# Batch 1's first graph layer run in lent tiles beside batch 0's later layers, nodes normalised in place, planner constants set anew

## The chip, the cores and the metric

The kernel runs on one core of one Trainium2 chip. The metric is the device time of one execution in microseconds, as a median of several runs. The core has TensorE (PE; its weight loads are PEld), VectorE (DVE), ScalarE (ACT), GpSimd (POOL) and SyncE (SP), which here only issues DMAs.

## The reference

Sixteen graphs (batches) of 1024 nodes with 256 features share one 0/1 adjacency matrix `adj`. Four layers follow each other, each with a normalisation ahead of it and a residual sum behind it:

```python
h = jnp.maximum(_layernorm(x, axis=-1), 0.0)
x = x + _L0_gnn_ref(h, adj, W0, a0)   # graph attention, 4 heads of 64
h = jnp.maximum(_layernorm(x, axis=-1), 0.0)
x = x + _L1_gnn_ref(h, adj, W1, a1)   # graph attention, 1 head of 256
h = jnp.maximum(_layernorm(x, axis=-1), 0.0)
x = x + _L2_gnn_ref(h, adj, W2, a2)   # graph attention, 1 head of 256
h = jnp.maximum(_layernorm(x, axis=-1), 0.0)
x = x + _L3_gnn_ref(h, adj, ...)      # 8 heads of 32 with q, k, v, then a feed-forward
# a graph layer:
q = h @ W; e = leaky_relu(q @ a_src + (q @ a_dst).T); e = where(adj > 0, e, -big)
out = act(softmax(e) @ q)
# the last layer:
t = softmax(where(adj > 0, q @ k.T / sqrt(32), -1e9)) @ v
y = layernorm(h + t); y = layernorm(y + relu(y @ w1 + b1) @ w2 + b2)
```

All of it is in float32. Only the kernel's branch `direct` matters here; another branch, `general`, isn't executed with these inputs.

## The kernel before

**Tiling.** A batch's 1024 nodes are eight tiles of 128, and most steps work on a half of four tiles (512 nodes). One half of a batch's nodes is one tile `xt` of a ring of three. For the last layer the normalised nodes go into halves `hna` of another ring of three, and the attention's result and the feed-forward's first normalisation are made in them.

**The stages of a batch.** `batch(b)` loads the nodes (L1537), takes their sums and squares on ACT (L1547, L429), runs `gat` for the three graph layers, writes the nodes to DRAM as `x3` (L1568), runs `attention`, then `feed`, which reads `x3` back as `xr` for the residual sum (L1444).

**A graph layer.** `gat` normalises a half into `hn` (ACT, L483), transposes it to `hT`, multiplies by the weights widened by the score columns (L716) and takes exponentials of the scores (L727). A leaky-ReLU softmax weight is then a maximum of a row and a column term: a row of scores is transposed, written to DRAM (`rd`, L789) and read back spread over all partitions (`row`, L797), and DVE makes each masked tile of weights `pt` from it in one instruction (L813). In the first layer, with four heads, TensorE multiplies in column-tiled form, four 32-column products side by side (L927), with the denominators (L937); in the other two one 257-column product does both (L840). One tile `qb` holds the projected nodes of a layer, so that a layer's products must be through before the next layer's projection writes it, whichever batch that is of.

**The attention.** `project` makes queries and keys of four heads (L1077), splits each into a high part `hi` (ACT, L1086) and a low part `lo` (DVE, L1089) of which there is one buffer each, and SP copies these by sixteen 64 KB DMAs into stacked tiles `ks` and `qs` (L1098). The 32 steps of a batch each make four score tiles `sc` (TensorE, L1295), their exponentials `pa` (ACT, L1319), the mask (DVE, L1328) and the products with the values in column-tiled form (L1161); the denominators come from sums of `pa`, partly by DVE (L1188), partly by accumulating DMAs from POOL's queue (L1196), and in the last batch from `pa` themselves. The four `sc` banks are taken in turn by scores, projections and transposes of this stage; four other PSUM banks serve everything else.

**The order.** Nothing is issued as the code runs. Every operation is put on record with its engine, an estimated duration, and what it reads and writes, and `schedule` then plays the program through: on each engine it takes, among the operations that can start soonest, the one with the lowest key, and issues them in that order. The key of an operation is its batch number plus a value between knots along the stage (`GATS`, `VALUES`, `STEPS`, `FEED`), less a `LEAD` for ACT and DVE. `SWITCH` is what a turn of TensorE between its kinds of products costs ("col4" is column-tiled, "qk" scores, "full" the rest); it is added to the duration, and times `BIAS` to the key when TensorE's next operation is chosen. A DMA takes its issue time on its queue, and its result counts as there when the queue's earlier transfers and its own are through, plus `LANDING`. On the chip each engine then does its list in this order, and waits where the plan was wrong.

Of the kernel before, what the change touches and what calls it, by code (L numbers as in the profile page):

```python
# [82 lines left out]

class Shared(Ring):
# [14 lines left out]
PASS = {"pe": 0.22, "act": 0.18, "dve": 0.15, "pool": 0.13, "dma": 0.0}  # L99


class Work:


    def __init__(self, engine, us, emit, key, modes, moved):
        self.engine, self.us, self.emit, self.key, self.modes = engine, us, emit, key, modes
        self.pass_on = PASS[engine]
        self.moved = moved
        self.before = {}
        self.after = []  # L110
        self.shared = []
        self.opens = []
        self.ready = 0.0
        self.left = 0
# [10 lines left out]
class Record:  # L125
# [12 lines left out]
    def add(self, engine, us, emit, w=(), r=(), modes=("full", "full"), key=None, moved=0.0):  # L138
        stream = self.streams[-1]
        x = Work(engine, us, frozen(emit), key, modes, moved)  # L140
# [29 lines left out]
    def schedule(self):  # L170
# [8 lines left out]
        queue = dict.fromkeys(PASS, 0.0)  # L179
# [22 lines left out]
        def choose(e):  # L202
# [10 lines left out]
            if future[e] and (best is None or future[e][0][0] < best[0]):  # L213
                t, n, x = future[e][0]
                if opening(x) is not None:
                    t = max(t, at, opening(x))
                    best = min(best or (1e9,), (t, x.key + turn(x), n, x))
# [3 lines left out]
        while True:  # L221
# [18 lines left out]
            if x.moved:  # L240
                queue[e] = max(at + 0.2, queue[e]) + x.moved
                x.pass_on = queue[e] + LANDING - (at + us)
# [17 lines left out]
LANDING = 2.8  # L260
BIAS = 0.939
LEAD = {"act": 2.715, "dve": 0.501}

SWITCH = {
    ("full", "col4"): 0.095,
    ("full", "col2"): 0.095,
    ("qk", "full"): 0.104,
    ("qk", "col4"): 0.2,
    ("qk", "col2"): 0.2,
    ("col4", "full"): 0.135,  # L270
    ("col4", "qk"): 0.135,
    ("col4", "col2"): 0.135,
    ("col2", "full"): 0.1,
    ("col2", "qk"): 0.1,
# [3 lines left out]
def act_us(n, pointers=0):  # L278
    return (n / 1.2 + 65 + 93 * pointers) / 1000


def tt_us(n):
    return (n / 0.96 + 73) / 1000


def stt_us(n):
    return (n / 0.96 + 130) / 1000


def ts_us(n):  # L290
    return (n / 0.96 + 56) / 1000


def mm_us(n):
    return 2 * max(2 * n / 2.4 + 2.3, 109) / 1000
# [5 lines left out]
def direct(ctx, tc, flag, x, adj, gat_w, gat_a, w_qkv, ln1_g, ln1_b, ln2_g, ln2_b, w1, b1, w2, b2, out):  # L301
# [10 lines left out]

    GATS = (
        (-3.456, -2.901, -1.928, -0.561, 0.293),
        (0.136, 0.471, 0.668, 0.738, 0.779),
        (0.851, 0.853, 0.845, 0.944, 1.195),
    )
    VALUES = (1.183, 1.195, 1.056, 1.638, 0.894)
    STEPS = (1.054, 1.508, 1.709, 1.977, 2.039)
    FEED = (2.172, 2.298, 2.316, 2.334, 2.401)  # L320
# [34 lines left out]
    r_xt = ring("xt", 3, [TH, C])  # L355
# [13 lines left out]
    r_hna = ring("hna", 3, [TH, C])  # L369
# [43 lines left out]
    def dma(moved, emit, w, r, key=None, us=0.44, engine="dma"):  # L413
        rec.add(engine, us, emit, w, r, key=key, moved=moved)

    def stats(src, src_ref, dst, dst_ref, whose="g"):
        st = r_st[whose].new()
        dve(0.342, lambda: nc.vector.bn_stats(st.t, src), [st], [src_ref])
        dve(0.11, lambda: nc.vector.bn_aggr(dst, st.t), [dst_ref], [st])
# [3 lines left out]
    def spread_of(srcs, src_refs, sums, squares, refs):  # L423

        act(0.19, lambda: nc.scalar.mul(sums, sums, -1.0 / C), refs, [])
        for k, (src, src_ref, ref) in enumerate(zip(srcs, src_refs, refs)):
            act(
                act_us(C, 1) + 60e-3,
# [51 lines left out]
    def normal(dst, dst_ref, src, src_ref, bias, scale, refs, func):  # L480
        act(
            act_us(C, 2),
# [5 lines left out]
    def watch(b_rec, view, k):  # L488
# [4 lines left out]
            0.3,  # L493
# [39 lines left out]
    def prepare(l):  # L533
# [5 lines left out]
            1.1,  # L539
# [7 lines left out]
            0.5,  # L547
            lambda: nc.sync.dma_start(
# [49 lines left out]
    def neighbours(it):  # L598
# [3 lines left out]
            1.9, lambda: nc.sync.dma_start(a_i, adj[it * P : (it + 1) * P, :]), [a32], []  # L602
# [39 lines left out]
    def setup():  # L642
# [3 lines left out]
        for it in range(NT):  # L646
# [5 lines left out]
            3.2,  # L652
            lambda: nc.sync.dma_start(wqkv_sb, w_qkv.rearrange("(t p) d -> p t d", p=P)),
# [12 lines left out]
        dma(5.0, load_feed, [b_feed], [], us=3.6)  # L666
# [4 lines left out]
    def gat(xt, b_mv, b_rstd, l):  # L671
# [3 lines left out]
        b_qb, b_e3, b_rec = r_qb.new(), r_e3.new(), r_rec.new()  # L675
# [4 lines left out]
        for hf in range(2):  # L680
# [5 lines left out]
            hn, hT = r_hn.new(), r_hT.new()  # L686
# [24 lines left out]
            for k, it in enumerate(its):  # L711
                g = r_bank.new()

                def project():
# [11 lines left out]
                    0.184,  # L726
# [30 lines left out]
            if H == 1:  # L757
                act(
                    0.17,
# [5 lines left out]
                0.4,  # L765
# [10 lines left out]
        def turn_rows(hf):  # L776

            g, rt, rd = r_bank.new(), r_rt.new(), r_rd.new()
# [9 lines left out]
            act(0.17, lambda: nc.scalar.copy(rt.t[:n, :], g.t[:n, :P]), [rt], [g])  # L788
            dma(0.15, lambda: nc.sync.dma_start(rd.t[:n, :], rt.t[:n, :]), [rd], [rt])  # L789
            return rd  # L790

        def spread(hf, h, rd):

            row = r_row.new()
            dma(
                1.4,
# [11 lines left out]
        def weights(hf, h, jt, row):  # L808

            pt = r_pt.new()  # L810
# [17 lines left out]
        for hf in range(2):  # L828
            s = slice(hf * TH, (hf + 1) * TH)
            if H == 1:  # L830
                row = spread(hf, 0, rds[hf])
                pts = [weights(hf, 0, jt, row) for jt in range(NT)]
                for k in range(TH):
                    it = hf * TH + k
                    g = r_bank.new()
                    for j0 in range(0, NT, PART):
# [22 lines left out]
                        0.116,  # L859
# [4 lines left out]
                    b_ex = r_ex.new()  # L864
# [7 lines left out]
                    if l != 1:  # L872
# [8 lines left out]
                            act_us(C),  # L881
# [10 lines left out]
                    else:  # L892
# [3 lines left out]
                        stt_us(C) + 60e-3,  # L896
# [15 lines left out]
            for h in range(0, H, 2):  # L912
                row = [spread(hf, h + u, rds[hf]) for u in range(2)]
                g, gd = r_bank.new(), r_bank.new()
                for jt in range(0, NT, 2):
# [7 lines left out]
                    def product():  # L923
# [23 lines left out]
                        3 * 0.855,  # L947
# [8 lines left out]
                for ac in (g, gd):  # L956
                    ot = r_ot.new()
# [13 lines left out]
                b_o, b_ex = r_ex.new(), r_ex.new()  # L971
# [5 lines left out]
                def sums():  # L977
# [9 lines left out]
                dve(0.13, lambda: nc.vector.reciprocal(r, r), [ref], [])  # L987
# [11 lines left out]
                act(act_us(HALF), lambda: nc.scalar.activation(ex, o, AF.Exp), [b_ex], [b_o])  # L999
                act(  # L1000
                    act_us(HALF),
# [25 lines left out]
    def attention(b, xt, b_mv, b_rstd):  # L1027
        rec.stream(b, VALUES)
        mv, rstd = b_mv.t, b_rstd.t
        hn, hT, va = Halves(r_hna), r_hTa.new(), r_va.new()  # L1030
# [39 lines left out]
        def project(g, hf, keys, stack, at):  # L1070
# [22 lines left out]
            for a in range(4):  # L1093
                part = ((hi, hi, lo, lo), (hi, lo, hi, lo))[keys][a]
                for r in range(HG):
                    dma(
                        0.33,
# [6 lines left out]
                        us=0.635,  # L1104
# [68 lines left out]
        rec.stream(b, STEPS)  # L1173
# [1017 lines left out]
```

## Time and profile before

| what | value |
|---|---|
| runs | 4154.15, 4158.94, 4161.55 us (median 4158.94) |
| span of the profiled execution | 4150.3 us |
| mean granted TensorE clock | 0.991 |
| busy, share of the span | PE 98%, PEld 57%, DVE 84%, ACT 65%, POOL 13% |
| DMA | 389.63 MB, 22.3% of the 16 engines' time from SP's queue, 16.0% from POOL's |
| scores of batch 0 | first end at 230 us |
| scores of batch 14 and 15 | 3740 to 3958 us, 3988 to 4110 us |
| from one batch's scores to the next | some 252 us |

The profiled execution is given by its span, from the first to the last instruction; the median of the runs lies 8.6 us above it. A busy time is the union of an engine's instructions in the trace. A matmul's row is as long as its stay in the pipeline, so that the rows of TensorE overlap; where it matters, the distance between the ends of two matmuls is used. A float32 product of the reference's full precision shows as two records.

### The profile page before, as it was taken

What the parts mean: (1) busy time and instruction counts of PE and PEld (TensorE: products, weight loads), DVE (VectorE), ACT (ScalarE), POOL (GpSimd) and SP (SyncE); (2) the same over time, 40 slices, a digit from 0 to 9 for tenths busy, and PEclk for the clock granted to TensorE, in tenths of its full rate; (3) what the DMA queues carried; (4) which work ended last, traced back from release to release, by engine and by line L of the source; (5) the groups of instructions that cost most, each with busy time, mean ns of one, the idle gap of its engine ahead of it and who ended that gap; (6) DMA issues with size and microseconds to landing.
All of it is one profiled execution on the core that took longest, in us unless ns stands there. A gap on an engine that the chain in (4) does not pass through costs nothing.

```text
span 4150.3 us, 68028 instructions
## 1 busy us (share of the span) xinstructions
PE 4049.7 (98%) x23874; PEld 2358.5 (57%) x23874; DVE 3504.5 (84%) x5994; ACT 2680.9 (65%) x6673; POOL 558.7 (13%) x631
## 2 busy tenths in 40 slices
PE   7899999999999999999999999999999999999998
PEld 3746556564665646556464665646556465564643
DVE  7498888988889898898988889888897988889866
ACT  4556667576766756667566665756667566575665
POOL 0001111111111101111111111111111111111110
PEclk9999999999999999999999999999999999999999
DMA  3124444344443424443254443434434244442441
GB/s 105 37 67 103 116 96 102 77 90 105 100 109 84 103 78 100 114 105 95 69 112 108 97 102 88 92 92 100 110 92 100 71 103 119 98 95 65 98 111 47
DMA packets 215246, 389.63 MB, mean 94 GB/s; under 512 B 45168, under 2 KB 80240, under 8 KB 214896
## 3 DMA queue, kind: packets, MB, share of 16 engines
q1 hardware_dynamic: 180336, 259.36, 22.3%
q0 software_dynamic: 34560, 125.84, 16.0%
q8 instruction: 190, 3.11, 0.3%
q14 instruction: 160, 1.31, 0.1%
HBM read 91.03 MB, written 33.95 MB: 30 GB/s over the span
## 4 chain that ended last, share of the span: by engine, by line
PE 79%; ACT 8%; DVE 6%; DMA 2%; SPq 2%; issue 2%; POOL 0%; DVEq 0%; ACTq 0%
PE bank L840 18%; PE bank L1161 12%; PE sc L1295 10%; PE bank L927 10%; PE bank L716 7%; PE bank L512 5%; PE bank L937 5%; PE bank L1392 5%; PE sc L1077 4%; ACT waste L429 2%; PE sc L1113 2%; SPq L1098 2%; DVE pa L1328 2%; ACT pa L1319 1%; DVE pt L813 1%
## 5 line engine op out<-in xcount | busy, mean ns | idle before, releaser
L1319 ACT ACTIVATE pa<-sc 128x512 f32<-128x512 f32 x2048 | 1108.1, 607 | 448.7 <-PE sc L1295 317.5
L1328 DVE TENSOR_TENSOR pa<-pa,mask 128x1024 f32<-128x1024 f32 x1024 | 1221.9, 1220 | 72.9 <-ACT pa L1319 68.6
L813 DVE SCALAR_TENSOR_TENSOR pt<-row,e,mask 128x512 f32<-128x512 f32 x1536 | 1068.1, 747 | 49.6 <-DMA row<-rd 35.8
L840 PE MATMUL bank<-qb,pt 128*128 128x257 f32 x4096 | 943.9, 383 | 1.4 <-DVE pt L813 1.0
L840 PEld LDWEIGHTS bank<-qb,pt 128*128 128x128 f32 x4096 | 780.5, 191 | 143.8 <-ACT pa L1319 11.7
L1295 PE MATMUL sc<-qs,ks 128*128 128x512 f32 x2048 | 702.8, 451 | 39.1 <-DVE lo L1089 35.7
L1295 PEld LDWEIGHTS sc<-qs,ks 128*128 128x128 f32 x2048 | 361.2, 190 | 288.1 <-issue 91.2
L1161 PE MATMUL bank<-pa,va 128*32 128x512 f32 x4096 | 514.7, 597 | 1.3 <-DVE pa L1328 1.0
L927 PE MATMUL bank<-pt,qb 128*32 128x512 f32 x4096 | 502.2, 596 | 4.3 <-DVE pt L813 3.4
L1188 DVE TENSOR_TENSOR sums<-pa,pa 128x1024 f32<-128x1024 f32 x360 | 435.6, 1221 | 30.3 <-PE bank L1161 25.3
L716 PE MATMUL bank<-w_aug,hT 128*128 128x259 f32 (+1 forms) x1536 | 391.2, 393 | 2.1 <-ACT hT L710 1.9
L1196 POOL DMA_DIRECT2D sums<-pa x240 | 210.5, 877 | 1059.4 <-DVE rec L860 239.0
L716 PEld LDWEIGHTS bank<-w_aug,hT 128*128 128x128 f32 x1536 | 283.9, 192 | 110.3 <-ACT pa L1319 12.6
L868 ACT ACTIVATE ex<-bank,rec 128x256 f32<-128x256 f32 x256 | 123.4, 482 | 303.3 <-DVE rec L860 302.6
L927 PEld LDWEIGHTS bank<-pt,qb 128*32 128x32 f32 x4096 | 122.3, 109 | 296.5 <-issue 224.0
L937 PE MATMUL bank<-pt,e 128*32 128x512 f32 x2048 | 278.6, 594 | 0.0
L1161 PEld LDWEIGHTS bank<-pa,va 128*32 128x32 f32 x4096 | 116.4, 109 | 256.7 <-issue 216.9
L1077 PE MATMUL sc<-hTa,wqkv_sb 128*128 128x512 f32 x512 | 244.5, 602 | 1.6 <-ACT pa L1319 0.8
L483 ACT ACTIVATE hn<-xt,mv,rstd 128x256 f32<-128x256 f32 x384 | 203.3, 597 | 51.6 <-DVE mv L456 30.0
L429 ACT ACTIVATE waste<-xt,mv 128x256 f32<-128x256 f32 x384 | 196.2, 511 | 7.0
L1161 PE MATMUL bank<-sums,ones 128*32 128x512 f32 x1440 | 193.5, 599 | 0.2 <-DMA sums<-pa 0.2
L1086 ACT CAST hi<-sc 128x512 fp32r<-128x512 f32 x128 | 74.5, 582 | 178.9 <-PE sc L1077 76.9
(119 smaller groups left out, 4305.9 us busy)
## 6 DMA issues: line engine op xcount, KB each, us to landing
sums<-pa POOLq DMA_DIRECT2D x240, 512.0 KB, 5.9
row<-rd SPq DMA_DIRECT2D x192, 256.0 KB
ks<-hi SPq DMA_DIRECT2D x512, 64.0 KB
ks<-lo SPq DMA_DIRECT2D x512, 64.0 KB
qs<-hi SPq DMA_DIRECT2D x512, 64.0 KB
qs<-lo SPq DMA_DIRECT2D x512, 64.0 KB
xt<-in_x_dram SPq DMA_DIRECT2D x32, 512.0 KB
x<-xt SPq DMA_DIRECT2D x32, 512.0 KB
```

What stands on the lines that cost most here:

```text
L429: lambda: nc.scalar.activation(waste.t, src, AF.Square, bias=sums[:, k : k + 1], accum_out=squares[:, k : k + 1]),
L716: nc.tensor.matmul(g.t[:, : C + 3 * H], hT.t[:, ct, k * P : (k + 1) * P], w_aug[l][:, ct, :], start=ct == 0, stop=ct == CT - 1,)
L813: lambda: nc.vector.scalar_tensor_tensor(pt.t, row.t, e3[:, 2, jt // TH, h, jt % TH : jt % TH + 1], mask[:, jt, hf * HALF : (hf + 1) * HAL ...
L840: nc.tensor.matmul(g.t[:, : D + 1], pts[jt].t[:, k * P : (k + 1) * P], qb[:, jt, 0, :], start=jt == 0, stop=jt == NT - 1,)
L927: nc.tensor.matmul(g.t[u * D + d : u * D + d + D3, :], qb[:, j, h + u, d : d + D3], pts[u][j - jt].t, start=j == 0, stop=j == NT - 1,)
L937: nc.tensor.matmul(gd.t[c : c + D3, :], one(jt + k, h + u).to_broadcast([P, D3]), pts[u][k].t, start=jt == 0, stop=jt == NT - 2,)
L1077: nc.tensor.matmul(sc.t, wqkv_sb[:, ct, c0 : c0 + P], hT.t[:, ct, hf * HALF : (hf + 1) * HALF], start=ct == 0, stop=ct == CT - 1,)
L1161: nc.tensor.matmul(ac.t[r * D3 : (r + 1) * D3, :], columns(r), of_head(r), start=first, stop=last,)
L1188: lambda: nc.vector.tensor_add(ss.t, p0.t, p1.t),
L1295: nc.tensor.matmul(scs[r - r0].t, ks.t[:, r, jt * P : (jt + 1) * P].bitcast(F32R), q.t[:, r, :].bitcast(F32R), start=True, stop=True,)
L1319: lambda: nc.scalar.activation(pt.t[:, v, :], sc.t, AF.Exp, scale=1.0 / math.sqrt(D3)),
L1328: lambda: nc.vector.tensor_mul(pt.t, pt.t, mask[:, jt : jt + 1, i0 : i0 + HALF].to_broadcast([P, 2, HALF]),),
```

## The change

It has four parts.

1. **The first graph layer of batch 1 in lent tiles.** `gat` takes its tiles from a set of rings `my`. `own` is the set as before. `lent()` makes another out of tiles that the attention and the feed-forward use (`va`, `hTa`, `xr`, `yT`, `fz`, `sums`, two of the six `pa`), which stand idle before the first attention. Batch 1's first layer is recorded right behind batch 0's, in the lent tiles, with knots of its own ("beside"); then the tiles are given back, and the next users of them wait for its instructions. Every later batch's layers use the own tiles, as before.
2. **Nodes in place.** `hna` is gone; `xt`'s ring has six halves and is named `xh`. The last layer's normalised nodes overwrite the nodes in `xh`, once the copy to `x3` has read them.
3. **The planner's model of a DMA.** SP and POOL share one queue of transfers, each transfer has its own landing time, and the issue of one takes as long as the queue is more than `AHEAD` = 3.5 us ahead. An operation that is to become ready may be taken ahead of an earlier one whose PSUM banks aren't free.
4. **New constants.** The estimated durations of operations, the cost of a turn, `BIAS`, `LEAD` and all knots are new; batch 15's feed-forward has knots of its own ("last").

The diff, cut to what matters:

```diff
+class Lent(Ring):
+    def __init__(self, tiles, owners):
+        super().__init__(tiles)
+        self.owners = owners
+    def new(self):
+        buf = super().new()
+        if len(self.bufs) <= len(self.tiles):
+            buf.parts[None][1] = [y for o in self.owners for y in o.parts[None][1]]
+        return buf
+    def give_back(self):
+        for o in self.owners:
+            o.uses += [y for buf in self.bufs for y in buf.uses]
...
             if future[e] and (best is None or future[e][0][0] < best[0]):
-                t, n, x = future[e][0]
-                if opening(x) is not None:
-                    t = max(t, at, opening(x))
-                    best = min(best or (1e9,), (t, x.key + turn(x), n, x))
+                for t, n, x in sorted(future[e]):
+                    if opening(x) is not None:
+                        t = max(t, at, opening(x))
+                        best = min(best or (1e9,), (t, x.key + turn(x), n, x))
+                        break
...
             if x.moved:
-                queue[e] = max(at + 0.2, queue[e]) + x.moved
-                x.pass_on = queue[e] + LANDING - (at + us)
+                queue = max(at + (us if e == "pool" else 0.2), queue) + x.moved
+                us = max(us, queue - at - AHEAD)
+                x.pass_on = queue + x.lands + SLACK - (at + us)
...
-LANDING = 2.8
-BIAS = 0.939
-LEAD = {"act": 2.715, "dve": 0.501}
+AHEAD = 3.5
+SLACK = 0.56
+KNOTS = {
+    "gat0": (-6.706, -3.534, -2.307, -1.522, -2.815),
+    "gat1": (0.005, 0.503, 0.618, 0.731, 0.916),
+    "gat2": (0.938, 0.468, 0.637, 0.867, 1.15),
+    "beside": (0.241, 1.203, 1.943, 0.54, 4.121),
+    "values": (1.06, -3.362, -0.305, 3.145, 0.767),
+    "steps": (1.014, 1.448, 1.59, 2.064, 1.794),
+    "feed": (2.016, 2.165, 2.509, 2.154, 2.609),
+    "last": (2.808, 3.335, 3.547, 5.206, 6.138),
+}
+BIAS = 1.225
+LEAD = {"act": 9.55, "dve": -0.732}
 SWITCH = {
-    ("full", "col4"): 0.095,
...
-    ("qk", "full"): 0.104,
-    ("qk", "col4"): 0.2,
...
-    ("col4", "full"): 0.135,
-    ("col4", "qk"): 0.135,
...
+    ("full", "col4"): 0.137,
+    ("col4", "full"): 0.18,
+    ("qk", "col4"): 0.15,
+    ("col4", "qk"): 0.184,
+    ("qk", "full"): 0.016,
 }
...
-    GATS = (
-        (-3.456, -2.901, -1.928, -0.561, 0.293),
-        (0.136, 0.471, 0.668, 0.738, 0.779),
-        (0.851, 0.853, 0.845, 0.944, 1.195),
-    )
-    VALUES = (1.183, 1.195, 1.056, 1.638, 0.894)
-    STEPS = (1.054, 1.508, 1.709, 1.977, 2.039)
-    FEED = (2.172, 2.298, 2.316, 2.334, 2.401)
...
-    r_xt = ring("xt", 3, [TH, C])
+    r_xh = ring("xh", 6, [TH, C])
...
-    r_hna = ring("hna", 3, [TH, C])
...
+    def lent():
+        va, hTa, xr = r_va.new(), r_hTa.new(), r_xr.new()
+        yT, fz, sums, pa = ([r.new() for _ in range(2)] for r in (r_yT, r_fz, r_sums, r_pa))
...
+        rings = types.SimpleNamespace(
+            qb=Lent([va.t.rearrange("p t c -> p (t c)")], [va]),
+            hn=Lent([wide[:, 0, :].rearrange("p (t c) -> p t c", c=C)], [hTa]),
+            hT=Lent([wide[:, 1, :].rearrange("p (t n) -> p t n", n=HALF)], [hTa]),
+            row=Lent(both(yT[:1]), yT[:1]),
...
+            rd=ring("rdl", 2, [P], dram),
+            pt=Lent(both(sums + pa), sums + pa),
+            ex=Lent(both(yT[1:]), yT[1:]),
+            ot=Lent([b.t for b in fz], fz),
+        )
+        return rings
...
-    def gat(xt, b_mv, b_rstd, l):
+    def gat(xt, b_mv, b_rstd, l, my):
...
-        b_qb, b_e3, b_rec = r_qb.new(), r_e3.new(), r_rec.new()
+        b_qb, b_e3, b_rec = my.qb.new(), my.e3.new(), my.rec.new()
...
     def attention(b, xt, b_mv, b_rstd):
-        hn, hT, va = Halves(r_hna), r_hTa.new(), r_va.new()
+        hn, hT, va = xt, r_hTa.new(), r_va.new()
...
     setup()
+    states = [begin(0), begin(1)]
+    graph(0, states[0], 0)
+    borrowed = lent()
+    graph(0, states[1], 0, borrowed, KNOTS["beside"])
+    for r in vars(borrowed).values():
+        if isinstance(r, Lent):
+            r.give_back()
     for b in range(NB):
-        batch(b)
+        if b > 1:
+            states.append(begin(b))
+        for l in range(int(b < 2), 3):
+            graph(b, states[b], l)
+        end(b, states[b])
```

`begin` is the first part of `batch` (load, sums, squares), `graph` sets the knots and calls `gat`, `end` is the rest: the copy to `x3`, `attention` and `feed`.

## The prediction, made before the change was run

> **What bounds the kernel now.** I read the page first, then the windows, then TensorE's own waits.
>
> ```profile
> PE 4049.7 (98%) x23874; PEld 2358.5 (57%) x23874; DVE 3504.5 (84%) x5994; ACT 2680.9 (65%) x6673; POOL 558.7 (13%) x631
> PE   7899999999999999999999999999999999999998
> DVE  7498888988889898898988889888897988889866
> PE 79%; ACT 8%; DVE 6%; DMA 2%; SPq 2%; issue 2%; POOL 0%; DVEq 0%; ACTq 0%
> ```
>
> TensorE bounds it: busy 98% of the span, 79% of the chain. But a busy row is not a full one. I multiply each matmul group's record count by the usual distance between ends in an unbroken run of it: 4096 x 217 ns (L840's, the second and third layer's products), 2048 x 232 ns (scores), 9888 column-tiled records (L927, L937, L1161: four heads or parts side by side, eight records of such a quad end within 0.85 us) at 107 ns, 1024 x 429 ns (L1077, L1392), 1024 x 219 and 512 x 226 ns (projections), 512 x 216 ns (values), 2720 transposes at 109 ns. That is 3825 us. So 4150 - 3825 = **325 us** is what a reordering could at best win. The windows show where it sits.
>
> ```profile
> 0.00:50.00 50.00, 31.65 (x182) 19.95 (x186) 36.23 (x84) 30.66 (x90) 5.14 (x12) 0.97 0.54 186
> 50.00:100.00 50.00, 46.27 (x357) 14.82 (x350) 42.24 (x79) 11.56 (x20) 1.01 (x1) 0.97 0.09 32
> 100.00:150.00 50.00, 43.19 (x194) 35.57 (x193) 20.73 (x59) 21.12 (x58) 3.41 (x6) 0.90 0.04 12
> 150.00:200.00 50.00, 45.62 (x194) 36.54 (x192) 21.75 (x60) 30.90 (x96) 3.49 (x6) 0.90 0.15 46
> 200.00:250.00 50.00, 47.92 (x321) 22.61 (x325) 38.13 (x65) 24.92 (x64) 3.26 (x5) 1.00 0.42 118
> 250.00:300.00 50.00, 48.27 (x340) 20.88 (x332) 49.05 (x79) 29.88 (x64) 6.25 (x4) 1.00 0.13 33
> 4000.00:4050.00 50.00, 46.98 (x262) 17.59 (x262) 37.15 (x44) 32.21 (x71) 1.72 (x2) 1.00 0.30 78
> ```
>
> Columns: stretch, busy time of PE, PEld, DVE, ACT, POOL (records), granted clock, DMA share, GB/s. By the same sum the first six stretches hold 23, 38, 39, 39, 45 and 42 us of dense work, so **73 us** are lost before 300 us. From 100 to 200 no engine is full (DVE 42 of 100): batch 0's second and third layer run alone, one dependent step after another. The last 150 us lose 39. The 213 us between are 14 us in each of 15 periods of 252 us. Two things make them up.
>
> First, one gap in each period, always in front of the scores:
>
> ```profile
> PE sc L1295 <- DVE lo L1089: 35.7, 14, 4.2
> ...
> 573.93 0.59 PE L1295 MATMUL sc<-qs,ks 128*128 128x512 f32 x1
> 577.90 1.65 PE L1295 MATMUL sc<-qs,ks 128*128 128x512 f32 x3 [3.38 <-DVE lo L1089]
> ...
> 564.62 0.58 SPq L797 DMA_DIRECT2D row<-rd  x1
> 565.24 0.45 SPq L1444 DMA_DIRECT2D xr<-x  x1
> 565.79 6.62 SPq L1098 DMA_DIRECT2D qs<-lo  x8
> 572.78 6.32 SPq L1098 DMA_DIRECT2D ks<-hi  x4
> ...
> 570.00:580.00 10.00, 6.62 (x24) 4.48 (x21) 5.85 (x9) 4.34 (x10) 2.26 (x3) 0.87 1.05 220
> 825.00:835.00 10.00, 6.30 (x20) 4.79 (x20) 5.11 (x11) 3.95 (x8) 1.72 (x2) 0.74 0.99 202
> ```
>
> The first line (TensorE's waits: total, times, longest) says 35.7 us over 14. The timeline and SP's queue say why: `lo` is one buffer, the eight qs<-lo transfers that read it were issued behind a row spread and an xr load while the 16 DMA engines were full (share 1.05), the next `lo` waits for them, it holds an `sc` bank, and the scores behind it in TensorE's queue wait. By ends of matmuls the fourteen gaps are 1.7 to 5.0 us, 44 in sum. Afterwards the clock drops: 0.87 and 0.74 of ten us lose 1.3 and 2.6 us. The mean clock of 0.991 is 37 us lost in all; 0.97, 0.90 and a last slice at 0.91 account for some 17, so about 20 belong to these gaps. Sum: **60 us**.
>
> Second, turns between column-tiled and other matmuls. An end after a turn into a quad comes 547 ns after the last, inside one 409: 138 ns. A turn out costs 180 to 200. I count 860 turns, 142 us.
>
> **What the Trainium skill says.** "Trainium Kernel Development and Optimization", Performance Expectations, calls matmul busy time a bad metric of the distance to the limit: the 98% over 3825 us of dense work agrees. Its Key Constraints say that SP's and POOL's DMAs run on the same 16 engines: the share of 1.05 where both are in flight agrees. "TensorE: Matmul & The Clock Gate", Part 1, says that the array falls to half clock after an idle window of some 3.4 us: the clocks above agree. The same part says that ScalarE's queue is strictly in order; I use it below.
>
> **The change, part by part.**
>
> *Batch 1's first layer in lent tiles.* No instruction is added: the layer's 64 weight rows x 0.747 us on DVE, its 256 + 128 column-tiled records (41 us) and projections (7 us) and transposes (3 us), some 55 us with the turns between them, move from 195-277 us into 100-240. SP's rd and row transfers of it move too, past an idle queue there (DMA share 0.04 and 0.15). Is there room? Until batch 0's layers and this one are done, PE needs 140 us (dense work up to 200) + 55 = 195, and loses 12.7 before its first matmul and some 23 more to the mask and batch 0's own first layer, where DVE (42 of 50) sets the pace and cannot take another layer. That is 231 us plus 5 of turns. DVE needs 36 + 42 + 42 + 60 = 180 in the same time, so it isn't the bound. Before, at 236 us, the kernel had done 139.6 + 36 x 0.9 = 172 us. Gain 195 - 172 = 23, and one us more where attention of batch 0 no longer shares DVE (49.05 of 50) with that layer: **24 us**; ends 5 (the lent layer stays bound to batch 0's DVE) and 35.
>
> *Planner's DMA model.* The old one gave SP and POOL a queue each and every transfer 2.8 us to land; the new one has one queue, its own landing for each transfer, and an issue that blocks when the queue is 3.5 us ahead. This names what made the gap: the scores will be placed later, with L840 products ahead of them (they follow at once in the timeline, so they were ready). Of 60 us I take **half, 30**: the transfers still need the same DMA time at a share of 1, and a new order has its own misses. Ends 0 and 60.
>
> *Turn prices and weights.* The price of a round trip full-quad-full goes from 0.939 x (0.095 + 0.135) = 0.22 to 1.225 x (0.137 + 0.18) = 0.39, of scores-quad-scores from 0.32 to 0.41. Dearer turns make longer runs, so fewer: I take 7% of 142, **10 us**; ends -15 (longer runs starve ACT's exp, 607 ns each, through the four sc banks) and 35.
>
> *Durations on ACT, DVE, POOL, and letting a ready item pass a closed one.* Order only; TensorE hides it (ACT 65%, DVE 84%). **0**, inside the ends above; without that cover it is the second rival.
>
> *Nodes in place, six halves.* Same memory (3 + 3 halves), same instructions. The new wait: the normal at L483 now overwrites what x<-xt (L1568) reads. In a steady period the write is issued at 1191.84, lands 4.61 us later by the chain, and the normal starts at 1201.39: 9.6 us after the issue, 5 to spare; the other half has 10. **0**; ends 0 and the second rival. A third batch's nodes can now be loaded, so the lead of one layer is kept to the end.
>
> *The end.* Batch 14's attention loses its companion first layer, 55 us, but keeps two layers and a feed-forward; batch 15's is alone in both, at 2.98 us a step, which is PE's 2.6 and one round of turns. The weights of the last feed may win some of the 13 us lost in 4000-4050. **0**; ends +10 and -10.
>
> Sum: 24 + 30 + 10 = 64 of the span, 4150.3 - 64 = 4086. The page gives the profiled execution only its span; the median of runs lies 8.6 us above it, so **4095 us**.
>
> **Rivals.** *All of it comes off (4029 to 4060):* 35 + 60 + 35 = 130 off. For it: every loss named has its cure in the planner. Against: the DMA share of 1.
>
> *Slower: the in-place wait.* If SP holds the x<-xt write behind two bursts of copies like those shown (6.6 + 6.3 = 12.9 us), it lands 12.9 + 4.6 - 9.6 = 7.9 us after the normal's turn. The normal stands in ScalarE's queue ahead of the exps, the four sc banks stay full, PE stops. It decides from 2 us in each of 32 halves, where it eats the 64. At 7.9 us in every third of them it costs 84 us: span 4170, runs **4179**. For it: the length of such bursts. Against: 5 us to spare, and a planner that knows of both.
>
> *The lead gives nothing:* DVE holds the lent layer, or it is paid back at the end, and 30 + 10 remain: **4119**. *Order changes, time doesn't:* new misses replace the old, some 10 off: **4149**, half of it within 0.2%.
>
> **How the numbers follow.** Forecast 0.53, all off 0.12, no lead 0.12, no change 0.08, slower 0.15. A measurement can tell 0.2% (8 us) from no change. Faster by more: 0.53 + 0.12 + 0.12 + a little of the fourth = 0.78; same 0.07; slower 0.15. The forecast's own range is 4065 to 4130. To leave out at most 2 in 10, the range goes down to half of the "all off" case, 4048, and up through no change to 4160.
>
> **What would show it.** Right: L927's column-tiled runs for a second batch between 100 and 240 us, clock 1.0 there; scores of batch 0 starting near 240 with second layers of batch 1 beside them; the wait of scores on `lo` below 18 us in sum; fewer than 860 turns; a period below 249 us. Wrong: a new line of ACT normal waiting for DMA x<-xt, a period at or over 252, or a tail of over 200 us after batch 14's last scores.

## The result, and the profile after

The changed kernel takes **4090.75 us** (median of four runs, 4087.86 to 4092.65) against 4158.71 for the kernel before (four runs, 4154.15 to 4161.55): ratio **0.9836, 95% interval 0.9824 to 0.9848**. Its profiled execution has a span of 4089.5 us and a time of its own of 4091.28 us, 1.8 above the span; the mean granted clock is 0.995. Lines of code have shifted: L840 is now L895, L927 L982, L1161 L1217, L1295 L1352, L1089 L1144, L1098 L1154, L483 L500.

The page after, busy times, slices and the shares of the chain:

```profile
PE 4023.3 (98%) x23874; PEld 2354.7 (58%) x23874; DVE 3499.0 (86%) x5994; ACT 2689.9 (66%) x6673; POOL 646.7 (16%) x631
PE   7999999999999999999999999999999999999998
DVE  7768898988979799897988989889797998979866
PE 85%; DVE 5%; ACT 4%; SPq 2%; DMA 2%; issue 1%; POOL 1%; DVEq 0%; ACTq 0%; POOLq 0%
```

As many instructions on every main engine as before; TensorE's share of the chain is up from 79% to 85%. Where the 60.8 us of the span come from is read off three marks, the first ends of the scores of batch 1 and of batch 14, and the end:

| stretch, us | before | after | gained | lost time before | after |
|---|---|---|---|---|---|
| to batch 1's first scores | 478.6 | 461.5 | 17.1 | 82.1 | 68.9 |
| thirteen periods, batch 1's to batch 14's scores | 3261.7 (250.9 each) | 3223.6 (248.0 each) | 38.1 | 185.3 | 137.2 |
| from there to the end | 410.0 | 404.4 | 5.6 | 60.0 | 60.5 |

Lost time is a stretch less its dense work: its matmul records, each at the usual distance between ends that the prediction lists. The two differ because the marks don't cut the same work. The new order does 9.9 us more dense work within the thirteen periods (48 column-tiled records more, and some transposes and feed-forward products), 3.8 less before them and 6.1 less behind them. So the periods lose 48.0 us less than before, the start 13.2 less, and the end has gained nothing: it only has less left to do.

The start, in the windows view after (columns: stretch, busy time of PE, PEld, DVE, ACT, POOL with records, granted clock, DMA share, GB/s):

```profile
50.00:100.00 50.00, 41.89 (x307) 19.09 (x300) 39.85 (x82) 22.88 (x66) 5.21 (x6) 0.93 0.14 41
100.00:150.00 50.00, 49.32 (x364) 23.47 (x365) 43.13 (x81) 18.03 (x43) 5.72 (x4) 0.97 0.10 33
150.00:200.00 50.00, 50.00 (x312) 32.11 (x315) 32.30 (x78) 23.99 (x65) 4.10 (x5) 1.00 0.06 17
200.00:250.00 50.00, 47.57 (x242) 36.00 (x235) 25.15 (x73) 28.25 (x76) 8.20 (x8) 0.99 0.20 63
```

From 100 to 200 us DVE is busy for 75 us instead of 42 and TensorE for 99 instead of 89: the lent layer fills the stretch in which batch 0 ran alone. From 50 to 100 TensorE has lost 4 us against before, though; e10 to e12 take that up.

The period, in TensorE's waits after (total, times, longest):

```profile
PE sc L1352 <- DMA qs<-lo: 5.8, 1, 5.8
PE sc L1352 <- DVE lo L1144: 4.4, 4, 1.7
```

The wait of scores on `lo` was 35.7 us in 14 and is 4.4 in 4. A gap is here what the distance between the ends of two matmuls has beyond the usual one (and beyond a turn). Between batch 1's and batch 14's scores, gaps of over 1 us fell from 36.2 us (13 of them) to 2.3 (2), and what matmuls lost by running at half clock fell from 11.1 us to none. The timeline after, at a place like the one in the prediction, and the window from 550 to 560 us with its DMA share (0.96):

```profile
547.68 7.04 SPq L1154 DMA_DIRECT2D qs<-lo  x8
553.60 0.82 PE L1352 MATMUL sc<-qs,ks 128*128 128x512 f32 x2
554.68 3.75 PE L895 MATMUL bank<-qb,pt 128*128 128x257 f32 x16 [0.27 <-ACT fz L1533]
558.07 0.82 PE L1352 MATMUL sc<-qs,ks 128*128 128x512 f32 x2
558.73 1.90 PE L895 MATMUL bank<-qb,pt 128*128 128x257 f32 x8
559.42 0.69 DVE L1144 TENSOR_TENSOR lo<-sc,hi 128x512 f32<-128x512 f32 x1 [0.99 <-issue]
560.28 0.82 PE L1352 MATMUL sc<-qs,ks 128*128 128x512 f32 x2
...
550.00:560.00 10.00, 9.73 (x43) 7.39 (x42) 9.01 (x12) 4.66 (x14) 2.50 (x3) 1.00 0.96 194
```

The burst of copies is still there (eight issues in 7.04 us, a share of 0.96), and the next `lo` is still late. What has changed is that TensorE has products of the other batch between the pairs of scores: a second- or third-layer product (L895) of eight or sixteen records stands where 3.38 us of nothing stood.

### The profile page after: what moved, and what is told of

Read it like the earlier page. It is cut to its first block, busy times and chain, and to the rows that moved or that the text cites. A ratio compares the mean times of both kernels' runs of the same rounds, so it can differ in the third digit from the quotient of the medians.

```text
span 4089.5 us, 68377 instructions
## 1 busy us (share of the span) xinstructions
PE 4023.3 (98%) x23874; PEld 2354.7 (58%) x23874; DVE 3499.0 (86%) x5994; ACT 2689.9 (66%) x6673; POOL 646.7 (16%) x631
## 4 chain that ended last, share of the span: by engine, by line
PE 85%; DVE 5%; ACT 4%; SPq 2%; DMA 2%; issue 1%; POOL 1%; DVEq 0%; ACTq 0%; POOLq 0%
PE bank L895 20%; PE bank L1217 14%; PE sc L1352 11%; PE bank L982 9%; PE bank L770 9%; PE bank L529 6%; PE bank L992 5%; PE bank L1449 4%; PE sc L1132 4%; PE sc L1169 2%; SPq L1154 2%; DVE pt L868 2%; DVE pa L1385 1%; POOL rstdz L466 1%; ACT waste L446 1%
## 5 line engine op out<-in xcount | busy, mean ns | idle before, releaser
L868 DVE SCALAR_TENSOR_TENSOR pt<-row,e,mask 128x512 f32<-128x512 f32 x1472 | 1016.3, 744 | 62.2 <-DMA row<-rd 40.3
L895 PE MATMUL bank<-qb,pt 128*128 128x257 f32 x4096 | 942.0, 380 | 3.5 <-ACT fz L1533 3.5
L895 PEld LDWEIGHTS bank<-qb,pt 128*128 128x128 f32 x4096 | 771.3, 189 | 147.1 <-ACT pa L1376 12.6
L1352 PE MATMUL sc<-qs,ks 128*128 128x512 f32 x2048 | 717.7, 455 | 11.2 <-DMA qs<-lo 5.8
L1217 PE MATMUL bank<-pa,va 128*32 128x512 f32 x4096 | 504.8, 596 | 0.3 <-DVE pa L1385 0.2
L1352 PEld LDWEIGHTS sc<-qs,ks 128*128 128x128 f32 x2048 | 360.4, 189 | 212.3 <-ACT pa L1376 56.5
L982 PE MATMUL bank<-pt,qb 128*32 128x512 f32 x3840 | 468.7, 597 | 2.4 <-DVE pt L868 1.4
L982 PEld LDWEIGHTS bank<-pt,qb 128*32 128x32 f32 x3840 | 118.8, 109 | 275.9 <-issue 193.0
L1217 PEld LDWEIGHTS bank<-pa,va 128*32 128x32 f32 x4096 | 120.5, 109 | 263.0 <-issue 227.6
L992 PE MATMUL bank<-pt,e 128*32 128x512 f32 x1920 | 258.5, 592 | 0.0
L500 ACT ACTIVATE hn<-xh,mv,rstd 128x256 f32<-128x256 f32 x376 | 195.9, 592 | 93.0 <-DVE mv L490 89.1
L466 POOL TENSOR_TENSOR rstd<-rstd,neg_half 128x4 f32<-128x4 f32 x96 | 138.5, 1443 | 597.0 <-DVE rstd L458 588.3
L820 POOL TENSOR_TENSOR sum_e<-sum_e,e 128x12 f32<-128x12 f32 (+1 forms) x94 | 114.7, 1220 | 648.2 <-ACT e L781 648.1
```

Of the source, the lines that this page charges most:

```text
L868: lambda: nc.vector.scalar_tensor_tensor(pt.t, row.t, e3[:, 2, jt // TH, h, jt % TH : jt % TH + 1], mask[:, jt, hf * HALF : (hf + 1) * HAL ...
L895: nc.tensor.matmul(g.t[:, : D + 1], pts[jt].t[:, k * P : (k + 1) * P], qb[:, jt, 0, :], start=jt == 0, stop=jt == NT - 1,)
L982: nc.tensor.matmul(g.t[u * D + d : u * D + d + D3, :], qb[:, j, h + u, d : d + D3], pts[u][j - jt].t, start=j == 0, stop=j == NT - 1,)
L992: nc.tensor.matmul(gd.t[c : c + D3, :], one(jt + k, h + u).to_broadcast([P, D3]), pts[u][k].t, start=jt == 0, stop=jt == NT - 2,)
L1217: nc.tensor.matmul(ac.t[r * D3 : (r + 1) * D3, :], columns(r), of_head(r), start=first, stop=last,)
L1352: nc.tensor.matmul(scs[r - r0].t, ks.t[:, r, jt * P : (jt + 1) * P].bitcast(F32R), q.t[:, r, :].bitcast(F32R), start=True, stop=True,)
```

## The experiments

**e1 to e4, one part undone or done alone.** The knots and everything else stay; the planner makes a new order from them.

```diff
 e1_no_lent (after; cut): every batch runs begin, graph 0..2 with its own tiles, end
-    graph(0, states[1], 0, borrowed, KNOTS["beside"])
 e2_old_dma (after; cut): a queue for each engine, 2.8 us for every landing, old issue times
-                queue = max(at + (us if e == "pool" else 0.2), queue) + x.moved
-                us = max(us, queue - at - AHEAD)
+                queue[e] = max(at + 0.2, queue[e]) + x.moved
 e3_old_turns (after)
-BIAS = 1.225
+BIAS = 0.939     # and the old SWITCH
 e4_dma_alone (before): the new model of DMAs, nothing else
```

> The changed kernel with batch 1's first layer back in the own tiles and the lead of one layer gone; in-place nodes, planner and knots stay. Theory (the lent layer is worth the start alone, about 17 us by the shift of batch 1's first scores from 479 to 462, and the gaps in the periods went because the planner now sees the DMAs): about 4091 + 17 = 4108, the period stays at 248 us and TensorE's wait of scores on lo stays below 10 us in sum. Rival (the lead of one layer gives the planner other work to put into the gaps): the period goes back to 251 and the wait on lo returns, 4108 + 38 = 4146.

> The changed kernel with the old model of a DMA (a queue for SP and one for POOL, 2.8 us to land, fixed issue times) and everything else new. Theory (the DMA model took the gaps away): the fourteen gaps return, 34 us of gaps over 1 us and 11 us of cold clock, less some 9 us of small gaps: 4091 + 36 = 4127, period 250.7, wait of scores on lo about 35 us. Rival (the new knots and turn prices took them away): 4091 within 6, no such wait.

> The changed kernel with the old prices of turns and the old weight of them (BIAS 0.939). Theory: turns go from 794 back to about 860, which at 0.165 us each is 11 us: 4102, no gaps over 1 us in the periods. Rival (turn prices are only a way to another order; their number doesn't matter): 4091 within 5 whatever the number of turns.

> The kernel before with the new model of a DMA alone, old knots, turns, durations and rings. Theory: the gaps of 1.7 to 5.0 us in front of the scores go, with their cold clock, 47 us of which some 9 come back as small gaps: 4159 - 36 = 4123, mean clock 0.995. Rival (knots): 4159 within 8, and the wait of scores on lo near 36 us.

| run | median, us | ratio to before [95%] | period, us | scores waiting on `lo`, us (times) |
|---|---|---|---|---|
| e1_no_lent | 4274.64 | 1.0282 [1.0268, 1.0296] | 259.9 | 8.8 (8) |
| e2_old_dma | 4321.48 | 1.0395 [1.0379, 1.0411] | 263.8 | 19.5 (15) |
| e3_old_turns | 4245.00 | 1.0211 [1.0197, 1.0224] | 258.0 | 2.4 (3) |
| e4_dma_alone | 4221.84 | 1.0155 [1.0141, 1.0169] | 255.9 | 10.0 (10) |

All four missed what theory and rival gave, by 63 to 194 us from the nearer of the two, and all to the slower side. Undoing parts that together brought 68 us cost 184, 231 and 154 us; these cannot be the prices of the parts. The waits show in part what happened. First e1, which in its steady periods does the same work as the changed kernel, then e3 (TensorE's waits of each):

```profile
PE bank L895 <- DVE pt L868: 21.4, 16, 1.5
PE sc L1352 <- ACT pa L1376: 15.0, 20, 1.2
```
```profile
PE sc L1357 <- ACT pa L1381: 19.1, 29, 1.2
```

Among the changed kernel's waits the scores' on `pa` is 0.5 us, once, and that of L895 on `pt` isn't listed. Turns came back as well: 932, 966, 1018 and 1066 in e1 to e4, where the changed kernel has 794 and the kernel before 860. At the 0.20 us that e9 below finds for one, the surplus over the kernel that each run started from is an estimated 28, 34, 45 and 41 us, in e4 the larger part of what it lost. Removing a layer from the first 240 us, or changing the price of a turn, sends the planner into another cycle for the batches after, with such waits and turns again and again. These knots fit one set of constants. What these runs do tell is the one sign that is not a time: with the new model of DMAs the wait on `lo` is small in e1, e3 and e4, with the old one it is not (e2). The clearest is e4, where nothing but the model differs from the kernel before: 35.7 us down to 10.0.

**e5 and e6, one part undone and the knots set anew.** In e5 the lent layer is away; the graph layers of batches 0 and 1 and batch 0's attention get their own knots, searched so that the later batches fall into the changed kernel's cycle again. In e6 the old model of DMAs is back, and all knots are searched for under it.

```diff
 e5_no_lent_first_knots (e1's kernel; cut)
-        rec.stream(b, knots or KNOTS[f"gat{l}"])
+        rec.stream(b, KNOTS[f"gat{l}_{b}"] if b < 2 else KNOTS[f"gat{l}"])
 e6_old_dma_searched (e2's kernel, one row of ten)
-    "beside": (0.241, 1.203, 1.943, 0.54, 4.121),
+    "beside": (0.818, 1.57, 2.172, 0.776, 4.357),
```

> The changed kernel without the lent layer, as e1, but with knots of their own for the graph layers of batches 0 and 1 and for batch 0's attention, searched in the planner so that the later batches fall into the changed kernel's order again; all knots of the later batches are the changed kernel's. Theory (in e1 the later order was lost, not the lead; the lent layer is worth the start alone): period 248, batch 1's first scores 13 to 20 us later than in the changed kernel, 4091 + 13 to 20 = 4104 to 4111. Rival (the period needs the lent layer): period over 250, 4130 or more.

> The changed kernel with the old model of a DMA, as e2, but with its knots searched anew under that model for some 25 minutes. Theory (a planner that doesn't see the DMAs leaves gaps in front of the scores whatever its knots are): wait of scores on lo of 20 us or more, period 250 or more, 4120 to 4150. Rival (any order that is searched for long enough is as good; e2 was slow because its knots were not): no such wait, period below 249, 4091 to 4105.

e5 took **4107.85 us** (0.9871 [0.9856, 0.9886]) with a period of 248.2 us, the changed kernel's cycle. What differs is nearly all at the start: batch 1's first scores come at 477.0 us against 461.5, with the same records behind them, 15.5 us; the thirteen periods differ by 3.3. So the lent layer is worth 4107.85 - 4090.75 = 17 us (15 by the ratios). The 17.1 of the first table only looks like that number: 3.8 of it is work moved past the mark, and e5 loses 2.3 us more than the kernel before at the start (84.4 against 82.1).

e6 took 4174.54 us (1.0034 [1.0022, 1.0045]), period 254.8. Its waits on TensorE:

```profile
PE bank L1210 <- DMA sums<-pa: 27.1, 19, 2.5
PE sc L1344 <- DVE lo L1138: 20.6, 28, 2.1
```

The theory's two signs hold (a wait on `lo` of 20 or more, a period of 250 or more), its time doesn't: the kernel takes 25 us more than the theory's upper end. Under the old model the waits on DMAs stay, by another name too: the denominators' products now wait for POOL's accumulating DMAs, which don't appear among the changed kernel's longest waits. How much of the 84 us over the changed kernel is the model's, and how much a shorter search, isn't settled.

**e7, the gap filled by hand in the kernel before.** The planner's old order is kept; in front of the second pair of scores of a step that follows a projection of queries, two groups of L840's products, one from just behind it and one from behind the next pair, are put ahead of it, 29 moves in all. Three pairs of scores then follow each other with nothing between.

```diff
-        for w in rec.schedule():
+        for w in earlier(rec.schedule(), 2):   # two ready products ahead of the tagged scores
```

> The kernel before in its own order, but for one move in each batch: two groups of L840 products (1.74 us each) are put ahead of the pair of scores that stood idle for lo (second pair of step (0, 1, 4)). Nothing else of the order changes, on no engine. Theory (the gap is idle time that ready products can fill, and with it the cold clock goes): of 44 us of gaps and some 19 us of cold clock at least 30 come off, 4159 - 30 to 45 = 4114 to 4129; wait of scores on lo below 10 us, mean clock 0.995 or more. Rival (the stretch is bound by DMA or ACT, so that the time comes back as waits of the next scores on their banks): 4159 within 10.

4141.18 us (0.9958 [0.9944, 0.9971]): 21 us off, not 30 to 45. Gaps of over 1 us fell from 36.2 to 1.2 us and half clock from 11.1 to 0, so the gap is gone, 46 us of it. But gaps of 0.2 to 1 us rose from 11 to 37 us. For 24 us they are scores that wait for ACT's exponentials `pa` to free their banks, where products stood between them before (in the waits view most of these are too short to be listed; TensorE's waits in e7):

```profile
PE sc L1326 <- ACT pa L1351: 7.4, 19, 0.9
PE sc L1326 <- DVE lo L1120: 3.8, 2, 2.9
```

So more than half of what this edit closed comes back a few matmuls later, since it took the products from between the next scores. In the changed kernel, where the whole cycle was planned round it, gaps of this size stand at 19 us.

**e8, the search carried on.** A plan that ends 6 us earlier in the planner's own reckoning, by a few knots and a `BIAS` of 1.29.

```diff
-BIAS = 1.225
+BIAS = 1.29
-    "beside": (0.241, 1.203, 1.943, 0.54, 4.121),
+    "beside": (0.241, 2.51, 1.943, 1.944, 4.121),
```

> The changed kernel with fourteen minutes more of the search over its knots and BIAS; nothing else. The plan ends 6 us earlier, mostly at the start. Theory (the plan is close enough to the chip now for such a gain to come through): 4085 within 4. Rival (the plan's misses are larger than its gains): 4091 or more.

4122.85 us (0.9908 [0.9892, 0.9923]), 32 us slower than the changed kernel; period 250.9, gaps of 0.2 to 1 us 38 us in sum instead of 19.

```profile
PE sc L1352 <- DVE lo L1144: 9.8, 13, 1.7
PE sc L1352 <- ACT pa L1376: 4.6, 17, 0.4
```

The rival holds: differences of 6 us between plans are below what the plan misses on the chip. That suggests that part of the changed kernel's 38 us is a plan that came out well.

**e9, turns added.** The changed kernel's own order, with 154 full products put between two column-tiled quads that stood side by side; turns go from 794 to 1076, and no other instruction changes its place among the rest.

```diff
-        for w in rec.schedule():
+        for w in split(rec.schedule()):   # quad, quad, full -> quad, full, quad
```

> The changed kernel in its own order, but for 154 places in batches 1 to 14 where two column-tiled quads and then another product follow each other: that product is put between the two quads. No work is added; turns into and out of column-tiled products go from 794 to 1076. Theory (a turn costs 138 ns in and 190 ns out wherever it stands, so the 66 turns that the change took away were worth 11 us): 141 pairs x 328 ns = 46 us, 4091 + 46 = 4137, within 10. Rival (turns lie in time that TensorE would lose anyway): 4091 to 4105.

4147.85 us (0.9966 [0.9954, 0.9978]): 57 us for 282 turns, **0.20 us each** (0.19 by the ratios). By distances of ends 45 us of it are the turns (0.16 each); the rest is new gaps of over 1 us (some 15 us, less what smaller gaps lost), such as this wait of TensorE in e9:

```profile
PE bank L560 <- DVE reca L1343: 12.1, 12, 1.0
```

"TensorEngine Tiling (Array Packing)" of the Trainium skill, Tiling Modes, says that a change of tiling mode drains TensorE. A turn's price agrees with a loss at each change: 0.16 us by itself here. The 66 turns that the change saves (860 to 794) are thus worth 11 to 13 us.

**e10 to e12, the start.** The ring of six halves lets batch 2's nodes be loaded from 36 us on, and the planner puts their sums and squares (ACT, L1607 and L446) ahead of what the lent layer needs: `hTa` below is its normalised nodes, since it borrows that tile. The timeline of the changed kernel:

```profile
48.58 0.42 ACT L1607 ACTIVATE waste<-xh 128x256 f32<-128x256 f32 x1
48.91 0.19 ACT L1607 ACTIVATION_READ_ACCUMULATOR waste<-xh 128x1 f32 x1
49.12 0.42 ACT L1607 ACTIVATE waste<-xh 128x256 f32<-128x256 f32 x1
...
54.36 0.17 DVE L458 TENSOR_SCALAR rstd<-mv 128x4 f32<-128x4 f32 x1 [4.67 <-ACT waste L446]
...
56.19 2.80 PE L529 MATMUL bank<-ident,hTa 128*128 128x128 f32 x8 [4.34 <-ACT hTa L500]
```

DVE waits 4.67 us for these statistics, TensorE 4.34, and from 54.3 us its clock is at half for 6.8 us. The three kernels put the 24 instructions (18 on ACT) behind the first 100 us, ACT's behind 150 and DVE's and POOL's behind 200, or ACT's one by one, 8 us apart, from 104 to 240 and the others behind 290.

```diff
-        for w in rec.schedule():
+        for w in later(rec.schedule(), rec.streams):   # batch 2's statistics held back
```

> The changed kernel in its own order, but for 24 instructions of ACT, DVE and POOL in the first 100 us: batch 2's sums and squares and the scale made from them, which the ring of six halves lets start at 45 us, are put behind everything planned up to 100 us. In the changed kernel's trace ACT works on them from 48.6 to 55.4 us, DVE stands 4.67 us idle for them in front of batch 0's weights, and TensorE 4.34 us. Theory (the start gained 17 us and not the 24 that was forecast because these statistics stand in front of batch 0's and the lent layer's work): 4 to 7 us off, 4084 to 4087, no gap over 4 us of TensorE between 50 and 60. Rival (DVE's work for two four-head layers sets the start's pace, so that the idle time is used up later): 4091 within 2.

> As e10, but the 24 instructions are kept apart: ACT's 18 of batch 2's statistics stand at 150 us of the plan, DVE's and POOL's 6 at 200. In e10 they stood together at 100 us, and DVE idled for ACT there again (2.34 and 2.40 us), with a gap of TensorE of 6.4 us at 110. Theory (the statistics' place is what the start lost): no gap of TensorE over 4 us between 50 and 250, batch 1's first scores 4 to 7 us before the changed kernel's 462, 4084 to 4087. Rival (DVE's pace over two four-head layers sets the start): 4091 within 3 though the gaps are gone.

> As e11, but ACT's 18 instructions of batch 2's statistics are set one by one, 8 us of the plan apart from 104 to 240 us, and DVE's and POOL's 6 stand at 290. In e11 the 18 stood together at 150 us, 10 us of ACT's time on end, DVE idled 5.65 us for the exponentials behind them and TensorE 3.2 us. Theory (the statistics cost the start only because they stand in one lump, wherever it is): no gap over 4 us of TensorE between 50 and 250, batch 1's first scores 3 to 6 us before the changed kernel's 462, 4085 to 4088. Rival (DVE's pace sets the start, and what is saved at 55 us is waited for later whatever the place): 4091 within 3.

e10: 4093.44 us (0.9841 [0.9828, 0.9855]); e11: 4092.66 (0.9845 [0.9832, 0.9859]); e12: **4088.31** (0.9832 [0.9819, 0.9846]). In the first two the gap moved with the block. e10's timeline, then e11's:

```profile
102.08 0.17 DVE L469 TENSOR_SCALAR rstd<-mv 128x4 f32<-128x4 f32 x1 [2.34 <-ACT waste L457]
109.43 3.62 PE L993 MATMUL bank<-pt,qb 128*32 128x512 f32 x13 [5.37 <-DVE pt L879]
```
```profile
159.89 0.42 DVE L965 SCALAR_TENSOR_TENSOR xh<-xh,ex 128x256 f32<-128x256 f32 x1 [5.65 <-ACT ex L936]
```

A block of 18 on ACT, some 10 us long, stopped what stood behind it in all three places. Spread out, no such stop is left. The longest gap between 50 and 250 us is then one of 3.1 us at 93 us, where TensorE waits for DVE's `rec`; with half clock after it, it is in the changed kernel too, at 100 us (e12's windows):

```profile
50.00:100.00 50.00, 46.01 (x342) 20.19 (x338) 45.13 (x88) 18.35 (x42) 3.46 (x4) 0.93 0.14 43
100.00:150.00 50.00, 50.00 (x367) 26.36 (x360) 41.48 (x88) 18.31 (x51) 6.67 (x5) 1.00 0.10 33
```

TensorE has 46.0 us instead of 41.9 in the first stretch, and batch 1's scores start at 459 instead of 462 us. The time is 2.4 us below the changed kernel's, and the intervals overlap: the trace shows 3 us gained at the start, the times can't confirm it. It is the lowest median of all kernels here.

## Why the prediction was right, and where it wasn't

**The sum.** 64 us of the span were forecast, 60.8 measured; of the medians 64 and 68, since adding 8.6 us to the span amounts to before's median less 64. Before's profiled execution was a quick one: with the 1.8 us that a timed run lies above its span it took some 4152.1 us, and of the 48 other timed runs of this kernel, beside e1 to e12, one is quicker (4150.14). The changed kernel's was close to its median. So some 7 of the 68 us stand in no comparison of the two profiles. That 64 came so near to 60.8 is in part luck. In lost time the start was forecast at 24 and gave 13.2, the periods at 30 + 10 and gave 48.0: one term too large and two too small cancel.

One count in the prediction is wrong: L927, L937 and L1161 have 11,936 column-tiled records, not 9888, which leaves L937 out. The sum of 3825 us goes with 11,936, so nothing that rests on it changes.

**The lent layer: 24 forecast, 17 measured, shown by e5.** The mechanism and the place were right (windows from 100 to 200). The term was too large. At 236 us, the moment for which the prediction reckons 195 us of dense work, the changed kernel has done 190 (before: 172, as reckoned). What was overlooked is the other use of the ring of six, batch 2's statistics on ACT ahead of the lent layer; e12 recovers about 3 of the 7 us. The forecast's 1 us for the first attention running without that layer did not come: between 225 and 300 us the lead in dense work shrinks from 17.6 to 11 us, and the first attention, with few other products to put between its quads, loses 12 us from 250 to 300, where the kernel before loses 8. How that could be mended was not tried. Two of the signs that the prediction named did not come as written: the clock from 100 to 150 us is 0.97, and batch 0's first scores end at 260 us, not near 240.

**"The lead of one layer is kept to the end" was wrong.** Batch 2's first-layer products run at 441 to 512 us beside batch 1's scores (462 to 666), the same phase as before (455 to 522 beside 479 to 682). From batch 0's scores to batch 1's it is 201 us instead of 248: there the lead is used up. From then on the phase is the old one, and the period is shortened by other causes. No number of the sum hung on this sentence.

**The DMA model: 30 of 60 forecast; gaps and clock gave 36 net.** The pool of 60 was somewhat too large. Its 44 us of gaps contain the 0.23 us that a score takes anyway, fourteen times; and of the clock's loss a part lies inside the gaps, where no matmul is there to be slowed. Gaps and slowed matmuls are 36.2 + 11.1 = 47 us in the thirteen periods and some 7 at the fourteenth place, 54 in all. Of the 47 us 45 went, and small gaps of 0.06 to 1 us grew by 9 (15.8 to 24.8). The halving was right for a local repair (e7: 46 gone, 26 back), too strict for a new plan of the whole cycle. That the planner's model decides about these gaps rests on the waits on `lo`: 35.7, 19.5 and 20.6 us under the old model (before, e2, e6), 2.4 to 10.0 under the new one (after, e1, e3, e4, e5, e8). That it brought the time is not shown: e4 has the model and not the knots, and is slower. The new durations, `LEAD` and the passing of a closed operation were not undone by themselves, and their share is open.

The half clock fits "TensorE: Matmul & The Clock Gate" of the Trainium skill, Part 1, in kind and not in its figure of an idle window of some 3.4 us: before, in the thirteen periods, it came after seven idle times of TensorE of 2.31 to 3.70 us, but not after two of 2.92 and 3.23 us. After, the longest gap in the thirteen periods is 1.2 us, and there is no half clock.

**Turns: 7% of 142 us forecast, 7.7% fewer, 11 to 13 us by e9's price.** In the thirteen periods their cost fell from 111.1 to 98.3 us. Together with the 36 that is 49 us, and the lost time fell by 48.0; of these 38.1 show in the length of the periods, the other 9.9 in the work that was moved into them.

**In place: 0 forecast, 0.7 us measured.** What the normal at L500 waited for in the whole run, by what released it:

```profile
  DVE mv L490: 91.7, 33
  DVE mv L473: 26.7, 17
  DMA x<-xh: 0.7, 1
```

One wait of 0.7 us: the second rival, the slower one, did not happen. What these halves alone would cost or bring was not tried.

**The end: 0 forecast, none gained.** The table's 5.6 us are 6.1 us of work less behind the mark; the lost time there is 60.0 us before and 60.5 after. The fourteenth gap on `lo`, 4.7 us at 3852 us, is gone, and a larger one has come in front of batch 15's first scores, the 5.8 us on qs<-lo shown above, at 3921 us.

## What to carry to other kernels

Where a planner orders a kernel, undoing one constant prices the fit of all others to it, not that constant: compare either after setting the knots anew (e5), or edit the finished order by hand (e7, e9, e12), which changes one thing only. A gap in front of the bound engine was worth a little under half its length where it was filled locally with products taken from close behind (e7), more where the cycle round it was planned anew, and the plan's own gain was no guide where it was smaller than the plan's misses (e8). When stretches of two orders are compared, compare the work in them too: here 10 us of it crossed the marks. When a ring of buffers grows, look at what the new slots let start early and ahead of whom: eighteen short instructions in a block stopped an engine that the same instructions, spread out, did not (e10 to e12).

## What the runs showed that was not expected

An accumulating activation is two instructions on ACT: above, 0.42 us for the sum and 0.19 for reading the accumulator, start to start 0.54 us (0.63 for the squares), where the planner had 0.40 and 0.50. The block of eighteen instructions, sixteen of them such, is 10 us of ACT's queue and not 8. And turns put into a finished order cost more than their own distances: 0.20 us in the time against 0.16 by the ends.
